# Product 5 of a convolution in two halves: 256-column units, then 512-column chunks of both sequences

## The chip, the cores and the metric

The kernel runs on one core of a Trainium2 chip. The metric is the device time in microseconds (us); lower is better. A core has a matrix engine (TensorE, PE in the profile; its weight loads are PEld), a vector engine (VectorE, DVE), an activation engine (ScalarE, ACT), a general engine (GpSimd, POOL) and a queue that issues most transfers (SyncE, SP). Matrix products are written to PSUM, which the kernel uses as 8 banks of 128 x 512 floats.

## The reference, cut to what matters

```python
x = x + attention(layernorm(x))          # x: 2 sequences x 1024 tokens x 1024
...
def attention(h):
    x = conv1d(h, conv_w, padding="SAME") + conv_b     # 3 taps, 1024 -> 768
    q, k, v = split(x, 3)
    # blocks of 128 tokens, 16 heads of 64, causal softmax, output projections
...
x = x + lora_linear(layernorm(x))        # 1024 -> 1024, 4 active experts
```

The change lies in the first third: the layer norm and the convolution with three taps over 1024 channels.

## The kernel before, in words

**The convolution as six products.** The tokens of each sequence are taken four at a time, and the convolution is computed from sums of shifted tokens times sums of taps, with six products per four tokens (numbered 0, 5, 1, 2, 3, 4 in the order they run) in place of twelve. Each product has 1024 input channels in 8 chunks of 128 (`NDC`), 768 output channels in 6 groups of 128 (`NCC`) and 256 columns for each of the two sequences (`J` = 256, `JN` = 512). A product therefore fills six PSUM banks, `pms[v, c]`, of 512 columns. For accuracy each operand is split into a rounded part and a remainder (`_hi` on ACT, `_lo` on DVE), and three matmuls stand for one: hi x hi, hi x lo, lo x hi (`three`).

**Two ways of multiplying.** Products 1 to 4 take a chunk of both sequences at once: 512 columns, 18 matmuls a chunk (`multiply`). Products 0 and 5 come first, while tokens are still being normalized and transposed, so they are cut into `units` (L464 on): one sequence, two chunks, 2 x 18 matmuls of 256 columns (`multiply_unit`). Units 0 to 7 are product 0, units 8 to 15 product 5. A unit's tokens are summed (`unit_sum`, DVE), rounded (`unit_hi`, ACT), and the remainder taken (`unit_lo`, DVE). Product 5 needs each chunk's weights for both sequences, so they stay in their buffers (a pool `t3` of 23) until the second sequence has passed.

**Tokens.** The input comes in 16 tiles of 128 tokens. Tiles 0 to 7 hold odd tokens (`xo`), tiles 8 to 15 even tokens (`xe`); 8 to 11 belong to the first sequence and 12 to 15 to the second. Each tile is normalized (statistics on DVE, scale on ACT) and transposed in two halves h = 0, 1 of 512 channels (chunks 0 to 3 and 4 to 7): a `turn(i, h)` is four PE transposes into a bank and one ACT copy (`transposed`, L399). The table `between` says after which half of which unit which turns come. Product 0 reads odd tokens only, product 5 even ones only, products 1 to 4 both.

**Products 1 to 4.** For products 1 and 2, and again for 3 and 4, DVE makes the sums of tokens of two chunks at a time, both sequences (`tokens_sum`, four instructions of 128 x 1024). Their `v_hi` and `v_lo` follow. The sums of taps are made by transfers that add to what is in place (`sum_g`, on POOL's queue) and by DVE (`combine`), then split by `u_hi` (ACT) and `u_lo` (DVE). A product's banks are emptied by ACT (`evacuate`) and stored (`spill`).

**The order.** Every step of the convolution is an `Op` with an engine, a planned time, a due time, a lead (how long ahead of its due time it may start) and the operations it waits for. `trace()` places them: over all engines it repeats the choice of the operation that can start earliest; on one engine, among those whose predecessors are placed, again the one that can start first, and of two equal ones the one due earlier. The instructions are then issued in the order of the planned starts, so on each engine this order is fixed; the chip runs it in order. An operation `tokens_sum` waits for `banks`, the list of all 32 copies of transposes. A second plan, after the convolution, orders attention and the second linear layer in the same way.

Of the kernel before, what the change touches and what calls it, by code (L numbers as in the profile page):

```python
# [10 lines left out]
F32 = mybir.dt.float32  # L11
# [5 lines left out]
ALU = mybir.AluOpType  # L17
# [22 lines left out]
def preln_block_kernel(  # L40
# [19 lines left out]
    nc = tc.nc  # L60
    N, L, D = x.shape
    C = conv_w.shape[2]
    NDC = D // P
    NCC = C // P
# [10 lines left out]
    J = L // 4  # L75
    JN = N * J
# [50 lines left out]
    def t4(name, shape, dt=FR):  # L127
        return t4p.tile([P, *shape], dt, tag="t4", name=name)
# [161 lines left out]
                t.append(sorted(places[k])[n - 1])  # L290
            return max(t, default=0.0)

    def trace():
        todo = {e: [o for o in plan if o.engine == e] for e in {o.engine: 0 for o in plan}}
        for ops in todo.values():
            ops.sort(key=lambda o: o.due)
        late = 0.0
        while any(todo.values()):
            best = None
            for e, ops in todo.items():  # L300
                held = None
                for o in ops:
                    t = o.earliest()
                    if t is None:
                        continue
                    t = max(free.get(e, 0.0), o.due - o.lead + late, t)
                    if o.port:
                        t = max(t, free.get("port", 0.0))
                    if held is None or t < held[0]:
                        held = (t, o)  # L310
                    if t <= free.get(e, 0.0):
                        break
                if held and (best is None or held[0] < best[0]):
                    best = held
            t, o = best
            o.start, o.end = t, t + o.takes
            free[o.engine] = o.end
            if o.port:
                free["port"] = o.end
            for k in o.need:  # L320
                places[k].remove(min(places[k]))
            for k in o.give:
                places[k].append(o.end + o.lag)
            todo[o.engine].remove(o)
            if o.engine == "PE":
                late = max(late, t - o.due)
        for o in sorted(plan, key=lambda o: o.start):
            o.f()
        plan.clear()
        return late  # L330
# [80 lines left out]
    raws, us, ukeep, vkeep, vts, pms = {}, {}, {}, {}, {}, {}  # L411
# [43 lines left out]
    def parts(dc, n):  # L455

        o, e = (
            t[:, dc, n, :] if isinstance(n, int) else t[:, dc].rearrange("p c n j -> p (c n) j")
            for t in (xo, home[0][0] if 0 in home else xo)
        )  # L460
        return (
            o[:, :, 0:J], e[:, :, 0:J], o[:, :, ds(J + 1, J)],
            e[:, :, ds(J + 1, J)], o[:, :, 1 : J + 1], e[:, :, 1 : J + 1],
        )  # L464


    units = [(v, n, dc) for v in (0, 5) for n in range(N) for dc in range(0, NDC, 2)]

    def unit_sum(q):

        v, n, dc = units[q]
        d = parts(ds(dc, 2), n)
        i = 0 if v == 0 else 1
        a = t2(f"va_{q}").rearrange("p (c j) -> p c j", c=2)
        nc.vector.scalar_tensor_tensor(a, d[i + 2], -5.0, d[i + 4], ALU.mult, ALU.add)
        nc.vector.scalar_tensor_tensor(a, d[i], 4.0, a, ALU.mult, ALU.add)
        vts[q] = a
# [6 lines left out]
    def unit_lo(q):  # L484
        a, vt = vts[q]
        nc.vector.tensor_tensor(vt[:, 1], a, vt[:, 0], ALU.subtract)
        vts[q] = [[vt[:, i, c, :] for i in range(2)] for c in range(2)]

    def tokens_sum(v, dc):


        d = parts(ds(dc, 2), None)
        a, b, kp = (t4(f"{n}_{v}_{dc}", (2 * N, J), F32) for n in ("va", "vb", "vkeep"))
        if v == 1:
            nc.vector.scalar_tensor_tensor(a, d[2], -4.0, d[4], ALU.mult, ALU.add)
            nc.vector.scalar_tensor_tensor(b, d[1], -4.0, d[3], ALU.mult, ALU.add)
            nc.vector.tensor_tensor(kp, a, b, ALU.subtract)
            nc.vector.tensor_tensor(a, a, b, ALU.add)
        else:
            nc.vector.tensor_tensor(a, d[4], d[2], ALU.subtract)  # L500
            nc.vector.tensor_tensor(b, d[3], d[1], ALU.subtract)
            nc.vector.scalar_tensor_tensor(kp, b, -2.0, a, ALU.mult, ALU.add)
            nc.vector.scalar_tensor_tensor(a, b, 2.0, a, ALU.mult, ALU.add)
        vkeep[v, dc], vkeep[v + 1, dc] = a, kp

    def v_hi(v, dc):
        hl = vts[v, dc] = [t4(f"v{i}_{v}_{dc}", (2 * N, J)) for i in range(2)]
# [26 lines left out]
    def mm(pm, v, dc, c, vt, first, last):  # L534
        three(pm, [u[:, ts(c, P)] for u in us[v, dc]], vt, first, last)

    def multiply_unit(q, i, c):
        v, n, dc = units[q]
        if (n, dc, i) == (0, 0, 0):
            pms[v, c] = bank(f"pm_{v}_{c}")  # L540
        mm(
            pms[v, c][:, ts(n, J)], v, dc + i, c, vts[q][i],
            dc + i == 0, dc + i == NDC - 1,
        )

    def multiply(v, dc, c):
        if dc == 0:
# [101 lines left out]
    HALF, TR = 2.15, 0.45  # L649
    DVE, ACT, PE, DMA = "DVE", "ACT", "PE", "DMA"  # L650
# [12 lines left out]
    at = [14.0]  # L663
    banks = []
    seen = {}
# [35 lines left out]
    for i in (6, 9):  # L701
# [9 lines left out]
    }  # L711

    idle = []
# [11 lines left out]
    last, ready = None, {}  # L725

    def evacuated(v, c, due):
        o = gone[v, c] = Op(ACT, 0.55 if v < 4 else 0.85, due, 3.0, [last], partial(evacuate, v, c))
        gone["m", v, c] = load(due, 3.0, spill, v, c, after=[o], takes=0.7)

    for q, (v, n, dc) in enumerate(units):
        base = 0 if v == 0 else 8
        took = [seen.get((base + 4 * n + i, dc // 4)) for i in range(4)]
        if None in took:
            for i in range(4):
                turn(base + 4 * n + i, dc // 4)
            took = [seen[base + 4 * n + i, dc // 4] for i in range(4)]
        due = at[0]
        if q == 0:

            Op(PE, 2.4, 16.9, 1.0, [seen["tr", 3, 0]], lambda: keep_busy(20))
        o = Op(DVE, 1.28, due - 5.5, 9.0, took, partial(unit_sum, q))
        o = Op(ACT, 0.55, due - 3.5, 9.0, [o], partial(unit_hi, q))
        side = Op(DVE, 0.64, due - 1.5, 9.0, [o], partial(unit_lo, q))
        for i in range(2):
            d = dc + i
            if n == 0:
                if v == 5:
                    gs[5, d] = load(at[0] - 12.0, 12.0, load_g, 5, d)
                ready[v, d] = weights_due(v, d, at[0], gs[v, d])  # L750
            for c in range(NCC):
                after = [last, side, ready[v, d]]
                if v == 5 and n == 0 and d == 0:
                    after.append(gone[0, max(0, c - 1)])
                last = Op(
                    PE, HALF / NCC, at[0], 6.0, after, partial(multiply_unit, q, i, c), lag=0.0
                )
                at[0] += HALF / NCC
            for j in between.get((q, i), []):
                turn(*j)  # L760
        if (n, dc) == (1, NDC - 2):
            for c in range(NCC):
                evacuated(v, c, at[0] + 0.1 * c)
    def begin_step(v, dc, due):
        if v in (1, 3):
            kept = Op(DVE, 4.7, due - 9.0, 22.0, banks, partial(tokens_sum, v, dc))
            gone["t", v, dc] = gone["t", v + 1, dc] = kept
        o = Op(ACT, 1.0, due - 5.0, 14.0, [gone["t", v, dc]], partial(v_hi, v, dc))
        return Op(DVE, 1.18, due - 3.0, 14.0, [o], partial(v_lo, v, dc))
# [31 lines left out]
    for v, dc in [(v, dc) for v in (1, 2, 3) for dc in range(0, NDC, 2)] + [(4, 0), (4, 2)]:  # L801
        if (v, dc) == (2, 0):

            for r in range(4):
                load(
                    at[0] + r, 3.0, nc.sync.dma_start, mask[r::4], causal[ts(r, P // 4)],
                    after=[last],
# [5 lines left out]
        for d in (dc, dc + 1):  # L813
            begin_chunk(v, d, at[0])
            for c in range(NCC):
                last = product(v, d, c, side)
# [14 lines left out]
    for c in range(NCC):  # L831
        got = load(
            at[0] - 4.0, 8.0, tokens_load, 0, c, t3, NV - 1,
            after=[gone["m", v, c] for v in (0, 5, 1, 2, 3)],
        )
        for d in range(NDC // 2, NDC):
            last = product(4, d, c, sides[d - d % 2])
        evacuated(4, c, at[0])
        o = Op(DVE, 2.7, at[0] + 1.0, 6.0, [got, gone[4, c]], partial(tokens_join, 0, c))
        o = Op(ACT, 0.6, at[0] + 4.0, 6.0, [o], partial(tokens_hi, 0, c))  # L840
# [3 lines left out]
    with tc.manual_schedule(  # L844
        engines={engines.DVE, engines.Activation, engines.PE, engines.SP, engines.Pool}
    ):
        nc.gpsimd.dma_start(bia, biases)
        Op(ACT, 0.2, 40.0, 3.0, [], lambda: nc.scalar.mul(bq8, bia[:, 0:NHP], SCALE))
        at[0] += trace()

    wqk, wvt, wot = par["wqk"], par["wv"], par["wo"]

# [576 lines left out]
    d = {}  # L1429
# [506 lines left out]
```

## Time and profile before

| | us |
|---|---|
| median of 3 runs | 752.37 (752.19 to 752.55) |
| the profiled execution | 752.35 |
| its span in the profile | 750.5 |
| first product to the end of product 4 (PE) | 18.78 to 230.03 |

| stretch, us | PE does |
|---|---|
| to 19 | transposes of tiles 0 to 3 and matmuls that only keep the engine busy |
| 19 to 61 | product 0, with transposes of tiles 4 to 11 |
| 61 to 99 | product 5, with transposes of tiles 12 to 15 |
| 99 to 230 | products 1, 2, 3, 4 |
| 230 to 750 | attention, output projection, the second layer norm and linear layer |

The span is what the profile records between the first and the last instruction; the rest of the time lies around it. A row of a timeline gives start, length (both us), engine, line, operation, the tile written and the tiles read, and in brackets how long the engine had been idle before it and what released it. Matmuls overlap, so their pace is read from the length of a run of them, not from the duration of one.

### The profile page before, as it was taken

The numbers are of one execution on the slowest core, as the hardware profiler recorded it, in microseconds if no ns is written. First come the engines' busy times: TensorE is split into PE (matmuls) and PEld (weight loads), VectorE is DVE, ScalarE is ACT, GpSimd is POOL, SyncE is SP. The second block draws the span as 40 slices with busy tenths as digits, with TensorE's granted clock in tenths as the row PEclk, the third lists the DMA queues.
The fourth block names the chain that finished last, engine by engine and source line by source line (L and its number), as shares of the span: only waits on it lengthen the run. The fifth ranks groups of instructions, "written<-read, shape, count | busy, mean of one in ns | idle before, by whom it ended". The sixth has DMA issues, their size and how long they took to land.

```text
span 750.5 us, 12939 instructions
## 1 busy us (share of the span) xinstructions
PE 741.9 (99%) x4746; PEld 633.9 (84%) x4746; DVE 596.3 (79%) x1051; ACT 421.3 (56%) x1044; POOL 187.4 (25%) x154
## 2 busy tenths in 40 slices
PE   8999999999999999999999999999999999999997
PEld 7999988888888888888888888888888888888886
DVE  6888899889767898898888888599667677577752
ACT  6888336464745998798898789863212212212120
POOL 3224321310000223132222312454142251331401
PEclk9999999999999999999999999999999999999999
DMA  9936994995753113363245344797655566565644
GB/s 342 379 104 206 248 267 107 292 287 124 249 167 127 44 50 103 132 220 103 99 153 206 131 151 138 266 386 317 227 211 225 215 238 235 209 225 217 227 174 168
DMA packets 65423, 149.46 MB, mean 199 GB/s; under 512 B 5918, under 2 KB 25006, under 8 KB 60240
## 3 DMA queue, kind: packets, MB, share of 16 engines
q1 hardware_dynamic: 61488, 138.51, 51.1%
q0 software_dynamic: 3728, 10.00, 7.4%
q8 instruction: 37, 0.61, 0.3%
q14 instruction: 26, 0.21, 0.1%
q10 hardware_dynamic: 144, 0.13, 0.1%
HBM read 114.01 MB, written 34.60 MB: 198 GB/s over the span
## 4 chain that ended last, share of the span: by engine, by line
PE 95%; DVE 2%; DMA 1%; ACT 1%; SPq 1%; issue 0%; DVEq 0%; ACTq 0%
PE pm L141 27%; PE pq L141 11%; PE py_c L1271 6%; PE pw L141 6%; PE py_a L1271 6%; PE pp L141 6%; PE py_e L1271 6%; PE pv L141 5%; PE po L978 4%; PE s L914 4%; PE pt L961 4%; PE py_b L1271 3%; PE pz L1288 2%; PE trx L1211 2%; PE tr L393 1%; DMA xt<-in_x 1%
## 5 line engine op out<-in xcount | busy, mean ns | idle before, releaser
L141 PE MATMUL pm<-v,u 128*128 128x256 f32 (+1 forms) x1152 | 203.1, 337 | 1.2 <-ACT v L481 0.6
L141 PEld LDWEIGHTS pm<-v,u 128*128 128x128 f32 x1152 | 177.8, 189 | 24.0 <-ACT v L481 0.9
L954 POOL TENSOR_TENSOR p<-p,rs 128x1024 f32<-128x1024 f32 x32 | 60.7, 1908 | 250.4 <-DVE rs L950 240.5
L943 ACT ACTIVATE p<-p,nmx 128x128 f32<-128x128 f32 x256 | 99.7, 398 | 4.3 <-DVE nmx L938 4.1
L141 PE MATMUL pq<-yt,wqk 128*128 128x512 f32 x384 | 94.6, 398 | 0.0
L141 PEld LDWEIGHTS pq<-yt,wqk 128*128 128x128 f32 x384 | 70.3, 188 | 16.8 <-issue 1.9
L1174 POOL TENSOR_TENSOR xr<-xr,projb 128x1024 f32<-128x1024 f32 x16 | 38.8, 2426 | 113.2 <-DMA xr<-in_x 104.7
L943 ACT ACTIVATION_READ_ACCUMULATOR p<-p,nmx 128x1 f32 x256 | 50.2, 196 | 0.0
L929 DVE TENSOR_TENSOR p<-s,mask 128x512 f32<-128x512 f32 x64 | 42.4, 685 | 9.7 <-PE s L914 9.5
L141 PE MATMUL pw<-oT,wot 128*128 128x512 f32 x192 | 47.9, 397 | 0.0
L141 PE MATMUL pv<-wvt,yt 128*128 128x512 f32 x192 | 47.1, 395 | 0.0
L141 PEld LDWEIGHTS pv<-wvt,yt 128*128 128x128 f32 x192 | 36.0, 188 | 8.8
L141 PEld LDWEIGHTS pw<-oT,wot 128*128 128x128 f32 x192 | 35.9, 188 | 8.7 <-DVE oT L999 0.2
L431 POOL DMA_DIRECT2D g<-in_conv_w x24 | 21.3, 938 | 69.9 <-ACT g L427 36.2
L453 DVE TENSOR_TENSOR u<-g,u 128x768 fp32r<-128x768 f32 x40 | 37.5, 953 | 1.5 <-ACT u L449 1.4
L969 DVE COPY pT<-pt 128x512 f32<-128x512 f32 x32 | 21.8, 688 | 20.8 <-PE pt L961 20.8
L938 DVE TENSOR_REDUCE nmx<-p 128x8 f32<-128x1024 f32 x32 | 37.7, 1196 | 0.1
L1233 ACT COPY s<-trx 128x512 f32<-128x512 f32 x8 | 4.7, 588 | 56.9 <-PE trx L1211 56.9
L449 ACT CAST u<-g 128x768 fp32r<-128x768 f32 x40 | 32.7, 838 | 5.2 <-PE pm L141 4.8
L914 PEld LDWEIGHTS s<-qk,qk 64*128 64x128 f32 x512 | 30.1, 187 | 5.1 <-issue 2.3
L914 PE MATMUL s<-qk,qk 64*128 64x128 f32 x512 | 34.0, 280 | 0.0
L1369 ACT COPY u<-py_a 128x512 f32<-128x512 f32 x8 | 4.7, 588 | 51.9 <-PE py_a L1271 51.9
(206 smaller groups left out, 1532.6 us busy)
## 6 DMA issues: line engine op xcount, KB each, us to landing
wb_B<-wsd_B SPq DMA_DIRECT2D x32, 1024.0 KB, 7.1
g<-in_conv_w SPq DMA_DIRECT2D x48, 384.0 KB, 8.3
mdr<-m SPq DMA_DIRECT2D x36, 256.0 KB, 3.0
g<-in_conv_w POOLq DMA_DIRECT2D x24, 384.0 KB, 7.3
xt<-in_x SPq DMA_DIRECT2D x16, 512.0 KB, 9.8
xr<-in_x SPq DMA_DIRECT2D x16, 512.0 KB, 5.6
out<-xr SPq DMA_DIRECT2D x14, 512.0 KB, 6.5
ml<-mdr SPq DMA_DIRECT2D x18, 384.0 KB, 4.0
```

Source lines behind the costliest of these rows:

```text
L141: nc.tensor.matmul(ps, l[a], r[b], start=first and i == 0, stop=last and i == 2)
L449: nc.scalar.copy(us[v, dc][0], raws[v, dc])
L453: nc.vector.tensor_tensor(lo, raws.pop((v, dc)), hi, ALU.subtract)
L914: nc.tensor.matmul(s[j][:, b, :], qh[ts(j, DH), ts(b, P)], kh[ts(j, DH), ts(b, P)], start=True, stop=True,)
L929: nc.vector.tensor_tensor(ps[i][0][:, ts(j, NB), :], ss[i][j], mask[:, None, :].to_broadcast([P, NB, P]), ALU.add,)
L938: nc.vector.tensor_reduce(nmx, p, AX.X, ALU.max, negate=True)
L943: nc.scalar.activation(p[:, k, :], p[:, k, :], AF.Exp, bias=nmx[:, k : k + 1], accum_out=sm[:, k : k + 1],)
L954: nc.gpsimd.tensor_tensor(p, p, rs[:, :, None].to_broadcast([P, 2 * NB, P]), ALU.mult)
L961: nc.tensor.transpose(pt[:, ts(b, P)], ps[i][0][:, j * NB + b, :], ident)
L978: nc.tensor.matmul(po[ts(j, DH), ts(b, P)], vh[:, b, ds((i % 4) * P + j * DH, DH)], pT[:, j, ts(b, P)], start=True, stop=True,)
L1174: nc.gpsimd.tensor_tensor(xrs[g], xrs[g], pwt["b"], ALU.add)
L1271: nc.tensor.matmul(pys[m, b], l[x], r[y], start=opens and c == 0 and i == 0, stop=c == NH - 1 and i == 2, skip_group_check=not opens,)
```

## The change

Product 5 now runs in two parts. Its chunks 0 to 3 stay in units of one sequence and two chunks (units 8 to 11). Its chunks 4 to 7 become four units of one chunk of both sequences, 18 matmuls of 512 columns each (units 12 to 15, sequence `None`). [...] The turns move: half 0 of tiles 12 to 15 comes at units 7 and 8, one at a time, and half 1 of all even tiles at units 9 and 10. A `tokens_sum` becomes two operations of two instructions each. And `trace` gets a patience: in the convolution an operation is only preferred to one that is due more than 2 us earlier if it can start over 1 us before it.

```diff
-    def trace():
+    def trace(wait=0.0):
...
-                    if held is None or t < held[0]:
-                        held = (t, o)
+                    if held is None or t < held[0] - (wait if o.due > due + 2.0 else 0.0):
+                        held, due = (t, o), o.due
                     if t <= free.get(e, 0.0):
                         break
...
-    units = [(v, n, dc) for v in (0, 5) for n in range(N) for dc in range(0, NDC, 2)]
+    units = [
+        *((0, n, dc) for n in range(N) for dc in range(0, NDC, 2)),
+        *((5, n, dc) for n in range(N) for dc in range(0, NDC // 2, 2)),
+        *((5, None, d) for d in range(NDC // 2, NDC)),
+    ]
...
-        d = parts(ds(dc, 2), n)
+        d = parts(ds(dc, 1 if n is None else 2), n)
...
-    def tokens_sum(v, dc):
+        if units[q][1] is None:
+            vts[q] = [[vt[:, i].rearrange("p c j -> p (c j)") for i in range(2)]]
+
+    def tokens_sum(v, dc, part):
...
+        if (v, part) == (1, 0):
+            stt(a, d[2], -4.0, d[4], ALU.mult, ALU.add)
+            stt(b, d[1], -4.0, d[3], ALU.mult, ALU.add)
+        elif v == 1:
+            tt(kp, a, b, ALU.subtract)
+            tt(a, a, b, ALU.add)
...
-        mm(
-            pms[v, c][:, ts(n, J)], v, dc + i, c, vts[q][i],
-            dc + i == 0, dc + i == NDC - 1,
-        )
+        cols = slice(0, JN) if n is None else ts(n, J)
+
+        opens = dc + i == 0 and (v == 0 or n == 0)
+        mm(pms[v, c][:, cols], v, dc + i, c, vts[q][i], opens, dc + i == NDC - 1)
...
-        (6, 1): [(8, 1), (9, 1)], (7, 0): [(10, 1), (11, 1)],
-        (9, 1): [(12, 0), (13, 0)], (10, 0): [(14, 0), (15, 0)],
-        (10, 1): [(12, 1), (13, 1)], (11, 0): [(14, 1), (15, 1)],
+        (7, 0): [(12, 0)], (7, 1): [(13, 0)], (8, 0): [(14, 0)], (8, 1): [(15, 0)],
+        (9, 0): [(8, 1), (9, 1)], (9, 1): [(10, 1), (11, 1)],
+        (10, 0): [(12, 1), (13, 1)], (10, 1): [(14, 1), (15, 1)],
...
+        which = range(base, base + 8) if n is None else range(base + 4 * n, base + 4 * n + 4)
+        took = [seen[i, dc // 4] for i in which]
...
-            kept = Op(DVE, 4.7, due - 9.0, 22.0, banks, partial(tokens_sum, v, dc))
+            kept = Op(DVE, 2.35, due - 9.0, 22.0, banks, partial(tokens_sum, v, dc, 0))
+            kept = Op(DVE, 2.35, due - 6.5, 22.0, [kept], partial(tokens_sum, v, dc, 1))
...
-        at[0] += trace()
+        at[0] += trace(1.0)
```

More of the change, by code (lines that the diff above doesn't have):

```diff
@@ L300, in trace @@
             for e, ops in todo.items():
-                held = None
+                held, due = None, 0.0
                 for o in ops:
@@ L487, in unit_lo @@
         vts[q] = [[vt[:, i, c, :] for i in range(2)] for c in range(2)]
-    def tokens_sum(v, dc):
+        if units[q][1] is None:
+            vts[q] = [[vt[:, i].rearrange("p c j -> p (c j)") for i in range(2)]]
+    def tokens_sum(v, dc, part):
         d = parts(ds(dc, 2), None)
[L493 to L498, printed above, removed]
-        else:
[L500 to L504, printed above, removed]
+        if part == 0:
+            vkeep[v, dc] = tuple(t4(f"{n}_{v}_{dc}", (2 * N, J), F32) for n in ("va", "vb", "vkeep"))
+        a, b, kp = vkeep[v, dc]
+        stt, tt = nc.vector.scalar_tensor_tensor, nc.vector.tensor_tensor
+        if (v, part) == (1, 0):
[4 more added lines that the diff above has]
+            tt(a, a, b, ALU.add)
+        elif part == 0:
+            tt(a, d[4], d[2], ALU.subtract)
+            tt(b, d[3], d[1], ALU.subtract)
+        else:
+            stt(kp, b, -2.0, a, ALU.mult, ALU.add)
+            stt(a, b, 2.0, a, ALU.mult, ALU.add)
+        if part == 1:
+            vkeep[v, dc], vkeep[v + 1, dc] = a, kp
     def v_hi(v, dc):
@@ L732, in preln_block_kernel @@
         base = 0 if v == 0 else 8
[L733 to L737, printed above, removed]
+        which = range(base, base + 8) if n is None else range(base + 4 * n, base + 4 * n + 4)
+        took = [seen[i, dc // 4] for i in which]
         due = at[0]
@@ L744, in preln_block_kernel @@
         side = Op(DVE, 0.64, due - 1.5, 9.0, [o], partial(unit_lo, q))
-        for i in range(2):
+        took = HALF / (3 if n is None else NCC)
+        for i in range(1 if n is None else 2):
             d = dc + i
-            if n == 0:
+            if n != 1:
                 if v == 5:
@@ L754, in preln_block_kernel @@
                     after.append(gone[0, max(0, c - 1)])
[L755 to L758, printed above, removed]
+                last = Op(PE, took, at[0], 6.0, after, partial(multiply_unit, q, i, c), lag=0.0)
+                at[0] += took
             for j in between.get((q, i), []):
                 turn(*j)
-        if (n, dc) == (1, NDC - 2):
+        if (n, dc) in ((1, NDC - 2), (None, NDC - 1)):
             for c in range(NCC):
```

## The prediction

> **What bounds the kernel now.** I read the busy shares first, then the groups of instructions, then the chain of waits, then the VectorE (DVE) and ScalarE (ACT) timelines around product 5, where the change lies.
>
> ```profile
> PE 741.9 (99%) x4746; PEld 633.9 (84%) x4746; DVE 596.3 (79%) x1051; ACT 421.3 (56%) x1044; POOL 187.4 (25%) x154
> ```
>
> TensorE (PE) is busy in 99% of the span. The view of who waited for whom lists only four PE waits in all: 2.9 us at the start, 0.6 and 0.5 us before the first product, 0.6 us at 260 us. So only fewer PE cycles can bring a gain, and a loss comes from any operand that is late. In the chain of waits (start us, length us, what) the stretch of the change reads:
>
> ```profile
> 59.15 10.79 PE pm L141 x90
> 69.94 0.87 PE tr L393 x8
> ...
> 79.12 0.87 PE tr L393 x8
> ...
> 79.99 150.04 PE pm L141 x738
> ```
>
> From 19.70 to 230.03 us the chain is nothing but PE: products, transposes, no gap. VectorE is what feeds it, by stretches of 30 us (us, PE, PEld, DVE, ACT, POOL, clock, DMA):
>
> ```profile
> 50.00:80.00 30.00, 30.00 (x257) 29.89 (x257) 23.92 (x41) 22.73 (x37) 10.92 (x14) 1.00 0.77 218
> 80.00:110.00 30.00, 30.00 (x210) 28.11 (x210) 28.96 (x30) 11.68 (x18) 7.04 (x8) 1.00 1.03 261
> 110.00:140.00 30.00, 30.00 (x134) 24.86 (x133) 29.19 (x40) 18.55 (x24) 7.28 (x8) 1.00 0.63 170
> ```
>
> DVE is 80% busy up to 80 us and 97% from 80 to 140 us. There it is nearly a second bound, so the question is when it may begin the work of product 1. These rows of the two timelines show that:
>
> ```profile
> 79.59 1.08 ACT L399 COPY xe<-tr 128x512 f32<-128x512 f32 x2 [1.43 <-PE tr L393]
> ```
>
> ```profile
> 80.70 0.69 DVE L475 SCALAR_TENSOR_TENSOR va<-xe 128x512 f32<-128x512 f32 x1 [1.81 <-ACT xe L399]
> 83.96 1.22 DVE L495 SCALAR_TENSOR_TENSOR va<-xo 128x1024 f32<-128x1024 f32 x1
> ...
> 111.10 1.22 DVE L495 SCALAR_TENSOR_TENSOR va<-xo 128x1024 f32<-128x1024 f32 x1
> 117.17 1.23 DVE L512 TENSOR_TENSOR v<-va,v 128x1024 fp32r<-128x1024 f32 x1 [0.26 <-ACT v L508]
> 118.32 0.95 DVE L453 TENSOR_TENSOR u<-g,u 128x768 fp32r<-128x768 f32 x1
> ```
>
> The last copy of a transpose ends at 79.59 + 1.08 = 80.67. Only then can the last units be summed, and the plan lets no `tokens_sum` start before all copies are done. From 83.96 to 123 us DVE is idle for 0.26 us in all.
>
> **Fewer matmuls.** Product 5 had 8 units of 36 matmuls of 256 columns. The second half of its chunks, 144 matmuls, becomes 72 of 512. The 256-column pace is 10.79 us / 90 = 119.9 ns. The last piece of the chain holds 9 x 18 = 162 of these, 19.42 us, and 576 of 512 columns, so those take (150.04 - 19.42)/576 = 226.8 ns. Two small ones cost 239.8 ns, one large one 226.8 ns: 72 x 13.0 ns = **0.93 us saved**, all on the path. [...]
>
> The second edit of the multiplication, no opening flag for the second sequence of product 5, costs nothing: the same matmul with another flag.
>
> **Transposes moved.** Product 1 of the old run starts at 79.99 + 19.42 = 99.41, the new one at 98.48. All 16 groups of the even tokens stay (8 transposes take 0.87). But the last group now stands before unit 11 and the four wide units, 4.32 + 16.33 = 20.65 us before product 1, so it ends at 77.83 and its copies 0.68 later, at 78.51 (before 80.67). Tiles 12 to 15 are needed at 57 to 65 us rather than 70 to 73. Their statistics run at 58.6 to 66.6 now and would have to move into 46 to 54. Beside them stand the splits of product 5's weights (four between 47.6 and 57.4), which are not read before 61 to 68 and can give way, and DVE idles 2.7 us there: nothing on the path. Price if that fails: one chain from statistics to scaled tile, some 4 us (1.65 for the statistics, 0.9 + 0.4 on POOL, 1.25 for the scale).
>
> **The switch from product 0 to 5.** Now tile 13 is transposed exactly there, and its copy stands in ACT's queue behind the first evacuation. The six evacuations ran from 59.72 at 0.51 us each with no stranger among them. With one 0.53 us copy in front of the other five, which waits for a transpose that ends near 60.4, evacuations two to five end at 61.5 to 63.0. PE wants its banks from 61.2 to 62.3 (0.36 us apart); two spare banks help, one of which the transpose holds. Between 0 and 0.85 us of stall; I take **0.4**.
>
> **The first wide unit.** Its sum can start at 78.51; the chain sum 1.33, the next sum 1.33 in front of its split, split 0.69, and 0.1 for signals gives 81.96, and PE comes at 77.83 + 4.32 = 82.15. It just fits: 0, at most 0.3.
>
> **VectorE in product 1.** Four units now need the last transposes where two did before. Start-to-start in DVE's timeline: a unit's sum 1.33, its split 0.61, a whole `tokens_sum` 4.83 (4.79 to 4.87), split of v 1.13, a combination of weights 0.87, split of u 0.87. From 78.51 to the point where chunk 6 of product 1 is ready: 4 x (1.33 + 0.61) + one late split of product 5's weights 0.87 + 4 x 4.83 + 4 x 1.13 + 8 x 0.87 + 7 x 0.87 = 45.5 us, thus 124.0. PE reaches chunk 6 (six chunks of 18 x 226.8 ns = 4.08 us) at 98.48 + 24.49 and reads the split in its second matmul, at 123.2. **Late by 0.8 us.** The old run by the same sum has 40.8 us from 80.67, 121.4 against 124.1: 2.7 us of room. That room is spent by two more units (3.9), a weight split (0.9) and the faster PE (0.9), less the 2.2 us by which the copies end earlier. DVE will be idle before 78 instead, about 10 us, since nothing else may start there.
>
> The two pieces help in order, not in amount. In the old run the sum at 111.10 (4.87 us) stood in front of the split at 118.32, used near 120.3. Divided, the second piece is due 0.1 us after that split, so the split moves ahead; chunk 5 is then ready at 118.7 against 119.3. Bounds of the product 1 stall: 0, if the last combination of weights goes behind and ACT is quick, to 2.1, if weight combinations hold the queue as well; I take **0.6**.
>
> **The plan's patience of 1 us.** It acts on the whole convolution. At the start it changes little: the operation worth waiting for is mostly not placed yet when DVE chooses, so the waits of 0.6 and 0.5 us stay (bounds: 0.3 gained, 0.3 lost). In product 3 the split at 176.05 is read near 177.4, with a `tokens_sum` at 171.26 in front; patience and pieces should bring it forward, which covers the 0.9 us by which PE comes earlier. Behind 230.03 nothing is edited; the plan there is made anew from the same relative times: 0, with ±0.5 for another order.
>
> **Sum**, against the profiled execution, 752.35 (span 750.5 and 1.85 around it): -0.93 + 0.4 + 0.6 = +0.07, hence **752.4 us**; the median of the runs shown, 752.37, is the same within 0.02.
>
> **Rivals.**
> *Clean gain.* No stall at the switch or in product 1: 752.35 - 0.93 = 751.4. For it: PE never waited between 20 and 230 us, ACT idles a lot, weights for product 1 can be loaded earlier since product 5 frees them earlier. Against it: the DVE sum.
> *Slower: the patience idles VectorE in product 1.* From 84 to 123 us DVE has no time to give. If the plan holds it for each of the four splits of v that wait for ACT (1.06 us for the cast plus signals, less one short operation that fits), 0.7 us each, all 2.8 us go to PE: 752.4 + 2.8 = 755.2. For it: the rule is blind to how loaded an engine is. Against: mostly a short operation with a near due time is ready, and the rule lets that go first. It decides from 1.4 us of such idling on (then the time is above 753.9).
> *The change doesn't do what it says.* If the wide units ran at twice the small pace, nothing is saved and the stalls stay: 753.3. Products 1 to 4 already run at the wide pace, so this is small.
>
> **Chances.** Forecast (0.4 to 1.8 us given back, 751.6 to 753.4) 0.42; clean gain 0.23; slower 0.30; no saving 0.05. The range 751.2 to 755.4 takes in the clean gain and the slower case's value. Faster by over 0.2% would need 1.5 us where 0.93 is to be had: 0.04. Within: 0.62. Slower: 0.34, the slower case and the upper end of the forecast.
>
> **What would show it.** Right: 72 fewer matmuls, product 5 shorter by 0.9; the last copy of the even tokens near 78.5; DVE idle between 54 and 78 and full after it; PE waits at L141 on DVE v or u between 115 and 125 us, and on ACT m near 61. Wrong: no PE wait at all there (751.4), or DVE idle between 84 and 123 with PE waits of over 2 us.

## The result, and the profile after

The changed kernel takes **757.28 us** (median of 5 runs, 755.91 to 757.6) where the kernel before takes 752.37. The ratio is 1.0054, with a 95% interval of 1.0043 to 1.0066: slower by 4.9 us, outside the range that was predicted (751.2 to 755.4). The profiled execution took 757.6 us, with a span of 755.8.

The busy shares of the page after the change:

```profile
PE 742.6 (98%) x4674; PEld 630.1 (83%) x4674; DVE 591.3 (78%) x1051; ACT 421.3 (56%) x1044; POOL 186.7 (25%) x154
```

The 72 matmuls are gone (4746 to 4674), so the change does what it says. The view by stretches (us, PE, PEld, DVE, ACT, POOL, clock, DMA share, GB/s) shows where PE lost time:

```profile
50.00:80.00 30.00, 29.87 (x250) 29.31 (x249) 19.82 (x34) 23.02 (x37) 7.55 (x12) 1.00 0.59 186
80.00:110.00 30.00, 27.77 (x132) 22.79 (x131) 26.13 (x30) 11.54 (x17) 8.96 (x11) 1.00 1.07 279
110.00:140.00 30.00, 27.68 (x119) 22.37 (x120) 28.21 (x39) 16.94 (x22) 5.13 (x6) 1.00 0.58 151
```

PE is idle for 2.2 and 2.3 us in the two later stretches, where it was never idle before. DVE does *less* between 80 and 110 us than it did (26.13, before 28.96), although the prediction had it as the full engine there. So something starved DVE. PE's own timeline names the operands that it waited for, in brackets ahead of which it was idle:

```profile
97.20 12.53 PE L141 MATMUL pm<-v,u 128*128 128x512 f32 x54 [1.96 <-DVE v L492]
110.75 0.50 PE L141 MATMUL pm<-v,u 128*128 128x512 f32 x1 [1.02 <-DVE v L526]
111.62 12.55 PE L141 MATMUL pm<-v,u 128*128 128x512 f32 x54 [0.37 <-DVE u L454]
125.37 4.83 PE L141 MATMUL pm<-v,u 128*128 128x512 f32 x20 [1.20 <-DVE u L454]
```

That is 4.55 us in four waits. The first is for the remainder of the last wide unit. The chain of waits (start, length, what) leads from it back to a transfer, where the old chain had only PE:

```profile
72.40 2.06 PE pm L141 x18
74.46 13.53 DMA g<-in_conv_w
...
88.81 0.62 ACT v L487
```

A load of weights (g) that PE's freeing of a buffer released at 74.46 us took 13.5 us. Three timelines tell why it came so late and whom it held. First SP, the queue that issues loads and stores:

```profile
44.69 0.33 SPq L421 DMA_DIRECT2D g<-in_conv_w  x1
60.68 4.59 SPq L544 DMA_DIRECT2D mdr<-m  x6
65.36 0.41 SPq L424 DMA_DIRECT2D g<-in_conv_w  x1
...
67.51 0.85 SPq L421 DMA_DIRECT2D g<-in_conv_w  x2
...
74.46 0.33 SPq L421 DMA_DIRECT2D g<-in_conv_w  x1
```

L421 loads weights for products 0 and 5, L424 and L425 for product 1, and L544 is the spill of a finished product. After 44.69 SP stands in front of product 0's spills and waits for their evacuation until 60.68. Everything behind them waits too: 10 loads are then issued within 5.2 us, and the last of product 5's, `g(5,7)`, stands behind eight of product 1's and waits for a buffer besides. In the kernel before, all eight loads of product 5 were issued by 51 us, ahead of the spills, as its row shows; here only five were.

```profile
24.62 26.39 SPq L420 DMA_DIRECT2D g<-in_conv_w  x8
```

Then ACT, which rounds the weights (L450) and the units (L487), and DVE:

```profile
78.04 1.07 ACT L400 COPY xe<-tr 128x512 f32<-128x512 f32 x2 [1.22 <-PE tr L394]
...
88.07 0.83 ACT L450 CAST u<-g 128x768 fp32r<-128x768 f32 x1 [5.51 <-DMA g<-in_conv_w]
88.81 1.14 ACT L487 CAST v<-va 128x512 fp32r<-128x512 f32 x2
```

```profile
85.07 0.69 DVE L482 SCALAR_TENSOR_TENSOR va<-xe,va 128x512 f32<-128x512 f32 x1
89.45 0.69 DVE L492 TENSOR_TENSOR v<-va,v 128x512 fp32r<-128x512 f32 x1 [3.70 <-ACT v L487]
...
96.46 0.68 DVE L492 TENSOR_TENSOR v<-va,v 128x512 fp32r<-128x512 f32 x1
```

The rounding of `g(5,7)` holds ACT for 5.51 us. The roundings of the last two wide units, whose sums were ready at 85.8, stand behind it; DVE stands idle for 3.70 us for want of them, and everything that DVE has to do for product 1 begins that much later. The remainder that PE waits for is made at 96.46, behind a sum for product 1.

A count by pace agrees. Unit 11 starts at 78.44 (counted as the prediction counted, from the end of the transposes ahead of it), 0.61 later than predicted. From there 36 matmuls of 119.9 ns and 648 of 226.8 ns would end at 229.72, but the convolution ends at 235.37: 5.65 us of stalls. Together with the 0.61 and less the 0.93 saved, that is the 5.3 us by which it ends later than before (230.03). The waits listed are 4.55 of it. The rest fits the last matmul ahead of each wait: on record it lasts 0.50 us (the row at 110.75), 0.27 more than the pace, and four times that is 1.1.

### The profile page after: what moved, and what is told of

The parts are those of the page before. It is cut to its first block, busy times and chain, and to the rows that moved or that the text cites. A ratio compares the mean times of both kernels' runs of the same rounds, so it can differ in the third digit from the quotient of the medians.

```text
span 755.8 us, 12795 instructions
## 1 busy us (share of the span) xinstructions
PE 742.6 (98%) x4674; PEld 630.1 (83%) x4674; DVE 591.3 (78%) x1051; ACT 421.3 (56%) x1044; POOL 186.7 (25%) x154
## 4 chain that ended last, share of the span: by engine, by line
PE 88%; DVE 6%; DMA 2%; ACT 1%; issue 1%; POOL 0%; DVEq 0%; ACTq 0%
PE pm L141 21%; PE pq L141 11%; PE py_c L1283 6%; PE pw L141 6%; PE py_a L1283 6%; PE pp L141 6%; PE py_e L1283 6%; PE pv L141 5%; PE po L990 4%; PE s L926 4%; PE pt L973 4%; PE py_b L1283 3%; PE pz L1300 2%; PE trx L1223 2%; DMA g<-in_conv_w 2%
## 5 line engine op out<-in xcount | busy, mean ns | idle before, releaser
L141 PE MATMUL pm<-v,u 128*128 128x512 f32 (+1 forms) x1080 | 204.4, 349 | 5.6 <-DVE v L492 2.9
L141 PEld LDWEIGHTS pm<-v,u 128*128 128x128 f32 x1080 | 174.2, 189 | 33.0 <-DVE v L492 3.5
L450 ACT CAST u<-g 128x768 fp32r<-128x768 f32 x40 | 32.6, 835 | 15.4 <-PE pm L141 7.8
```

Of the source, the lines that this page charges most:

```text
L141: nc.tensor.matmul(ps, l[a], r[b], start=first and i == 0, stop=last and i == 2)
L450: nc.scalar.copy(us[v, dc][0], raws[v, dc])
```

## The experiments

Ratios are to the kernel before, measured on the same chip beside each group of runs, with their 95% intervals. The kernel before had medians of 752.48 (x runs), 752.83 (y runs) and 753.27 (z runs), so times of different groups are compared by their ratios. The fastest executions of the kernel before agree in all three groups (751.75, 751.86 and 751.85); what moves its median is their scatter, up to 756.8. The ratios contain that scatter, so where they and the medians of the runs disagree, both are given.

### The loads of product 5's weights

**x1**: the changed kernel, with the loads of the four wide chunks due 22 us earlier, ahead of the spills.

```diff
-gs[5, d] = load(at[0] - 12.0, 12.0, load_g, 5, d)
+gs[5, d] = load(at[0] - (34.0 if n is None else 12.0), 12.0, load_g, 5, d)
```

> The changed kernel, but the four weight loads of product 5's chunks 4 to 7 are due 34 us before their chunk instead of 12, so that SP issues them ahead of product 0's six spills, as the kernel before did. Theory A (blocked queue: the load of chunk 7's weights comes late, its rounding on ACT stands in front of two roundings of token sums, and VectorE idles 3.7 us behind it): VectorE's idle of 3.7 us near 86 to 89 us is gone and about 3.7 us come back, 753.6 +- 0.8. Theory B (patience of 1 us orders product 1 badly): no more than 1 us comes back, 756.3 to 757.3. Theory C (the prediction's: too much VectorE work after the last transposes): the idle may go, and what is left over the kernel before is PE waits in product 1 of 0.8 to 2 us; 752.2 to 754.

Measured: 754.34 us, ratio 1.0026 [1.0017, 1.0034]. 2.9 of the 4.9 us are back by the medians; by the ratios, whose excess falls from 0.54% to 0.26%, about half of the loss. This lies in theory A's range. SP's timeline of this run has all eight loads of product 5 ahead of the spills:

```profile
24.91 18.16 SPq L421 DMA_DIRECT2D g<-in_conv_w  x8
60.92 4.29 SPq L544 DMA_DIRECT2D mdr<-m  x6
```

DVE is then full from 79.40 to past 126 us but for 0.39 and 0.25 us, and the wait of 1.96 is gone. PE's timeline has two left in product 1, 1.66 us in all, within the 0.8 to 2 of theory C:

```profile
108.58 12.53 PE L141 MATMUL pm<-v,u 128*128 128x512 f32 x54 [0.37 <-DVE u L454]
122.41 7.77 PE L141 MATMUL pm<-v,u 128*128 128x512 f32 x33 [1.29 <-DVE u L454]
```

**x2**: the loads as in the changed kernel; only the rounding of `g(5,7)` may no longer be placed early, so that the units' roundings go first.

```diff
-o = Op(ACT, 0.76, due - 5.0, 12.0, [after], partial(u_hi, v, d))
+o = Op(ACT, 0.76, due - 5.0, 3.0 if (v, d) == (5, 7) else 12.0, [after], partial(u_hi, v, d))
```

> The changed kernel with one number changed: the rounding of chunk 7's weights in product 5 may start at most 3 us ahead of its due time instead of 12, so ACT's queue has it behind the roundings of units 14 and 15. The load itself stays late (lands near 88 us). Theory A: the late load then hurts nobody, the same 3.7 us come back as in the run with early loads, 753.6 +- 0.8. If it is instead the saturated transfers (late weights of product 1) that hurt: no gain, 757.

Measured: 756.2, ratio 1.0045 [1.0032, 1.0058]. Theory A fails here: the idle of 3.70 is gone, and yet only 1.1 us came back by the medians, and the interval overlaps that of the changed kernel. The loads of product 1 that stand in the same burst now hold DVE (2.05 us at 106.52), and PE waits for it:

```profile
110.94 0.50 PE L141 MATMUL pm<-v,u 128*128 128x512 f32 x1 [1.63 <-DVE v L526]
```

So the blocked queue on ACT is one of two ways in which the late loads act. x1 takes away the first and most of the second (DVE stands 0.39 us there). How much of the lateness of `g(5,7)` is the blocked SP, the wait for a buffer or the slow landing was not tested separately.

### The patience

**x3**: the changed kernel without patience.

```diff
-at[0] += trace(1.0)
+at[0] += trace()
```

> The changed kernel with the patience of trace() set back to 0. Theory B: most of the 4.9 us come back, 752.4 to 753.5. Theory A: ACT's queue still has chunk 7's rounding in front of roundings of token sums, and the load is as late: 756 to 758.5, and the PE waits in product 1 stay.

Measured: 755.69, ratio 1.0043 [1.003, 1.0056], 1.6 us back by the medians, between the two theories and with an interval that overlaps that of the changed kernel. Besides, this run can't be read for patience alone: the plan also orders the loads otherwise, `g(5,7)` lands at 82.7 in place of 88.0, and DVE idles only 1.77 us for it. Therefore **z1**: x1 without patience, with the loads early in both.

> x1_loads_before_spills with the plan's patience taken out: the weight loads of the wide chunks stand ahead of the spills in both, so the load order that blurred x3_no_patience should differ less. Theory (patience is harmless or helps a little): 754.3, within 0.5 of x1 (754.34). Rival (patience idles VectorE or ACT for the sake of later operations): 1 us or more back, 753.3 or less.

Measured: 753.96, ratio 1.0008 [0.9999, 1.0017], against x1's 1.0026. The profiled executions differ by 0.9 (753.74 and 754.65), the ratios by 1.3 us, the medians of the two groups by 0.4. By the medians this is the theory, by the ratios the rival. Where it comes from is to be seen in the order on DVE. With patience (x1), ahead of the split that PE waits for at 122.41:

```profile
118.15 1.22 DVE L509 TENSOR_TENSOR vkeep<-va,vb 128x1024 f32<-128x1024 f32 x1
119.39 1.23 DVE L510 TENSOR_TENSOR va<-va,vb 128x1024 f32<-128x1024 f32 x1
120.54 0.95 DVE L440 SCALAR_TENSOR_TENSOR g<-g,g 128x768 f32<-128x768 f32 x1
121.41 0.95 DVE L454 TENSOR_TENSOR u<-g,u 128x768 fp32r<-128x768 f32 x1
```

and without it (z1):

```profile
118.05 1.23 DVE L510 TENSOR_TENSOR va<-va,vb 128x1024 f32<-128x1024 f32 x1
119.20 0.95 DVE L454 TENSOR_TENSOR u<-g,u 128x768 fp32r<-128x768 f32 x1
120.06 0.95 DVE L440 SCALAR_TENSOR_TENSOR g<-g,g 128x768 f32<-128x768 f32 x1
```

The split comes 2.2 us earlier. Most of it is accounted for: 0.87 since a combination of weights no longer stands in front of it, 0.64 since DVE no longer idles 0.39 and 0.25, 0.44 since the whole stretch began earlier. PE then waits 0.36 us in product 1. So patience does cost, between 0.4 and 1.3 us, and by the order of the operations more than by an idle engine. z1 has a wait of 0.69 us at 231.18 in return, for an evacuation behind product 4.

### The pieces

**x4**: the kernel before, with the sums in two pieces and with patience, but with small units throughout.

> The kernel before with the tokens' sums in two pieces and the patience of 1 us, but with product 5 in its old units and the transposes in their old places. Theory A and C: the loss belongs to the wide units, so this one is at 752.4 +- 0.7. Theory B: slower by 2 us or more.

Measured: 753.31, ratio 1.0015 [1.0, 1.0029]. Its trace has no wait in product 1. Most of the 4.9 us therefore needs the wide units or the turns that moved with them, which this run leaves out together.

**z2**: x1 with the sums whole again.

```diff
-kept = Op(DVE, 2.35, due - 9.0, 22.0, banks, partial(tokens_sum, v, dc, 0))
-kept = Op(DVE, 2.35, due - 6.5, 22.0, [kept], partial(tokens_sum, v, dc, 1))
+kept = Op(DVE, 4.7, due - 9.0, 22.0, banks, lambda: [tokens_sum(v, dc, k) for k in range(2)])
```

> x1_loads_before_spills with the sums of the tokens' side planned as one operation again. Theory (the pieces do not bring the split of chunk 5 of product 1 ahead, since its combination of weights is planned late): same time as x1, 754.3 within 0.5, and the PE wait on DVE u near 122 us stays near 1.3 us. Rival (the prediction's: the pieces hold the wait down): that wait grows by 1 us or more and the time goes to 755.3 or above.

Measured: 757.1, ratio 1.0047 [1.0032, 1.0062]. The theory falls: the pieces help, by 1.6 us by the ratios and 2.8 by the medians, part of which is a lower clock after the wait (0.57 from 112 to 116 us in the profiled execution; last section). The place is another one, as PE's timeline shows:

```profile
110.67 0.50 PE L141 MATMUL pm<-v,u 128*128 128x512 f32 x1 [3.26 <-DVE v L526]
```

The whole sum at 104.61 stands in front of the split of v of chunks 2 and 3 (109.40), and PE waits 3.26 us for that. In x1 that split goes between the two pieces of this sum (106.45) and costs PE nothing there.

### The width alone

**z3**: x1 with only chunks 6 and 7 wide, and the turns of the even tokens behind units 6 to 10, none at the switch between products.

```diff
-*((5, n, dc) for n in range(N) for dc in range(0, NDC // 2, 2)),
-*((5, None, d) for d in range(NDC // 2, NDC)),
+*((5, n, dc) for n in range(N) for dc in range(0, NDC - 2, 2)),
+*((5, None, d) for d in range(NDC - 2, NDC)),
...
-(7, 0): [(12, 0)], (7, 1): [(13, 0)], (8, 0): [(14, 0)], (8, 1): [(15, 0)],
-(9, 0): [(8, 1), (9, 1)], (9, 1): [(10, 1), (11, 1)],
-(10, 0): [(12, 1), (13, 1)], (10, 1): [(14, 1), (15, 1)],
+(6, 1): [(8, 1), (9, 1)], (7, 0): [(10, 1), (11, 1)],
+(8, 1): [(12, 0), (13, 0)], (9, 0): [(14, 0), (15, 0)],
+(9, 1): [(12, 1), (13, 1)], (10, 0): [(14, 1), (15, 1)],
```

> x1_loads_before_spills with only chunks 6 and 7 of product 5 multiplied wide, the even tokens' turns back behind units 6 to 10 (none at the switch from product 0 to 5, as in the kernel before). Expected saving of PE time half of 0.93 us, 0.46. Theory (the loss of x1 is the switch, about 0.9, plus VectorE's lateness in product 1): the switch costs nothing again and two more units, not four, need the last transposes, whose copies end about as early: 752.0 to 752.8, same as before. Rival (the pieces and the patience cost by themselves, as x4_before_pieces_patience's 0.8 hints): 753 to 754.

Measured: 752.34 us (751.9 to 752.74, 11 runs), ratio 0.9984 [0.9975, 0.9993], as its theory said. This is the fastest version of the study: about 5 us below the changed kernel, and 0.16% below the kernel before, which had 753.27 beside it. The interval leaves out 1, but the margin is smaller than the 0.2% from which the prediction counts a kernel as faster, and the profiled execution (752.5) is no faster than that of the kernel before (752.35). Nor is its fastest one (751.9, against 751.85); what is smaller is the scatter. z3 changes the number of wide chunks and the turns together, so it doesn't tell which of the two made x1's loss go. From 50 to 140 us PE has no wait:

```profile
80.00:110.00 30.00, 30.00 (x179) 26.82 (x178) 29.73 (x31) 11.51 (x16) 8.56 (x10) 1.00 1.07 271
110.00:140.00 30.00, 30.00 (x134) 24.82 (x133) 26.70 (x37) 18.29 (x24) 5.20 (x6) 1.00 0.57 155
```

**z4**: z3 with whole sums and no patience.

> z3_two_wide_chunks with whole sums and no patience: the kernel before with two wide chunks, earlier turns and early loads only. If the wide chunks as such are harmless: 751.9 (752.4 less 0.46), at most the same as before. If turns or loads collide anyway: 753 or more, with PE waits on ACT m or DVE u to show where.

Measured: 756.91, ratio 1.0039 [1.0026, 1.0051]. The first alternative misses by 5 us, and the second holds. With two wide chunks, pieces and patience *together* are worth 4.6 us by the medians, a lower clock among it (the profiled execution has two spells, with 0.50 and 0.64 in the stretches of 2 us from 20 to 24 us and 0.84, 0.50 and 0.81 in those from 104 to 110). PE waits 1.95 us at 104.56 for an evacuation of product 5. The evacuations (103.92 on) stand on ACT behind a rounding at 102.24 that waited 7.92 us for a whole sum on DVE. In z3 the plan puts the evacuations (96.41) ahead of that rounding (100.30).

### The switch from product 0 to product 5

**y1** and **y4** are x1 with the turns at the switch elsewhere.

```diff
-(7, 0): [(12, 0)], (7, 1): [(13, 0)], (8, 0): [(14, 0)], (8, 1): [(15, 0)],
+(7, 0): [(12, 0), (13, 0)], (8, 1): [(14, 0), (15, 0)],
```

> The run with early loads (754.34), and no transposes at the switch from product 0 to product 5: tile 13 is turned together with tile 12 in unit 7, tiles 14 and 15 together after unit 8; the last transposes stay where they are. If the copy among the evacuations costs what the trace shows there (about 0.9 us between 60 and 66 us), 0.9 us come back: 753.4, and PE starts unit 11 about 0.9 us earlier. If that delay only lets VectorE catch up (it works off the same amount before product 1 whatever PE does), the waits in product 1 grow by the same 0.9 us and the time stays at 754.3.

```diff
-(7, 0): [(12, 0)], (7, 1): [(13, 0)], (8, 0): [(14, 0)], (8, 1): [(15, 0)],
-(9, 0): [(8, 1), (9, 1)], (9, 1): [(10, 1), (11, 1)],
-(10, 0): [(12, 1), (13, 1)], (10, 1): [(14, 1), (15, 1)],
+(7, 0): [(12, 0), (13, 0)], (8, 0): [(14, 0), (15, 0)],
+(8, 1): [(8, 1), (9, 1)], (9, 0): [(10, 1), (11, 1)],
+(9, 1): [(12, 1), (13, 1)], (10, 0): [(14, 1), (15, 1)],
```

> The run with early loads, all turns of the even tiles earlier: tiles 12 and 13 in unit 7, 14 and 15 after the first half of unit 8, and the last transposes after the first half of unit 10 instead of its second half, with none at the switch. The last copies end about 2.2 us earlier, 77 instead of 79.4. Theory C with the switch: 0.9 us at the switch and the 1.7 us of waits in product 1 go, 751.4 to 752.2, at or below the kernel before. If VectorE's start does not decide: 753.4.

Measured: 755.64, ratio 1.0034 [1.002, 1.0048], and 755.74, ratio 1.0033 [1.0019, 1.0048]. Both are misses, 1.3 and 1.4 us worse than x1 by the medians (0.6 and 0.5 by the ratios). In y1 the scale of tile 15 (59.85) now stands in front of the evacuations on ACT, the sixth evacuation waits 2.40 us for the landing of a spill, and the last copy ends later, not earlier (80.73, against 79.37 in x1). In y4 the scales again stand there (57.50 and 59.59, the evacuations from 61.46), and PE waits 0.56 and 0.85 us for evacuations. Moving two turns moves their statistics and scales as well, to where ACT is busy with the evacuations (61.00 to 63.52 in y1, 61.46 to 64.01 in y4, for the first five). The cost of the switch itself was therefore not isolated; the pace count gives about 0.9 us for it in the changed kernel.

### DVE's room in product 1

**y2**: x1 with one subtraction less in each of the four sums of product 1. The kernel leaves out the difference that product 2 needs and multiplies `b` in its place, so it serves for its time alone.

```diff
-tt(kp, a, b, ALU.subtract)
...
-vkeep[v, dc], vkeep[v + 1, dc] = a, kp
+vkeep[v, dc], vkeep[v + 1, dc] = a, b if v == 1 else kp
```

> The run with early loads, and VectorE spared four instructions of 1.25 us in product 1: the difference that product 2 uses is left out (product 2 multiplies one of the two sums instead). Theory C (VectorE has too much work after the last transposes): three of them stand before the split that PE waits for at 122.4, so that PE wait of 1.3 us and the one of 0.4 us vanish, 752.6 +- 0.4. If the waits come from weights that land late, not from VectorE's load: no gain, 754.3.

Measured: 753.07, ratio 0.9992 [0.9978, 1.0005]. With 5 us less for DVE to do, 1.3 us come back by the medians (2.6 us by the ratios), and the wait of 1.29 at 122 us is gone. Waits of 0.44 and 0.36 us near 108 stay, for a split of v and one of u on DVE; why these come late with less for DVE to do is not shown.

**y3**: the kernel *before*, with that subtraction issued twice in three of the sums, 3.7 us more for DVE.

```diff
-nc.vector.tensor_tensor(kp, a, b, ALU.subtract)
+for _ in range(2 if dc < 6 else 1):
+    nc.vector.tensor_tensor(kp, a, b, ALU.subtract)
```

> The kernel before, with one instruction of each of the first three sums of product 1's tokens issued twice (3 x 1.25 = 3.7 us more for VectorE between 84 and 107 us, the same order of all instructions). The prediction's sum gives the kernel before 2.7 us of room at chunk 6, its trace about 1.0 us at the split for chunk 5. So theory C: PE waits 1.0 to 2.7 us in product 1, 753.4 to 755.1. If VectorE's load in product 1 does not matter: 752.4.

Measured: 756.45, ratio 1.0043 [1.0026, 1.006]. The kernel before has almost no room: two of the three extra subtractions (2.5 us) are done by 103 us, and PE waits 2.17 us there, for an evacuation that stands on ACT behind a rounding that waits for DVE. In the kernel before, ACT had the same order, without a wait of PE:

```profile
98.13 1.06 ACT L508 CAST v<-va 128x1024 fp32r<-128x1024 f32 x1 [6.61 <-DVE va L498]
99.83 3.03 ACT L524 ACTIVATE m<-pm 128x512 f32<-128x512 f32 x6
```

In y3 the chain of waits has the rounding at 100.93 and the evacuation that PE waited for from 102.71. PE's timeline of y3, and the stretches around it:

```profile
103.26 5.07 PE L141 MATMUL pm<-v,u 128*128 128x512 f32 x14 [2.17 <-ACT m L525]
```

```profile
102.00:104.00 2.00, 0.74 (x3) 0.66 (x4) 2.00 (x3) 2.00 (x4) 0.87 (x1) 1.00 1.06 263
104.00:106.00 2.00, 2.00 (x7) 1.52 (x7) 2.00 (x3) 2.00 (x5) 0.88 (x1) 0.59 1.04 332
106.00:108.00 2.00, 2.00 (x7) 1.57 (x6) 1.97 (x3) 0.36 (x1) 0.00 (x0) 0.56 1.08 297
108.00:110.00 2.00, 2.00 (x10) 1.62 (x9) 1.97 (x2) 0.00 (x0) 0.87 (x1) 1.00 1.08 294
```

The wait isn't all: after it PE runs 7 matmuls in 2 us in place of 10, at a granted clock of 0.59 and 0.56. That is another (0.41 + 0.44) x 2 = 1.7 us, so the 4.2 us by which this execution (756.57) is longer than that of the kernel before are 2.17 of wait, 1.7 of clock and 0.3 of the rest, which fits the 0.27 of a last matmul ahead of a wait.

## Why the prediction was wrong, by its own steps

The step that failed is the one on VectorE in product 1: it summed DVE's work and took for granted that DVE is fed. In the measured run DVE stood idle for 3.70 us instead, behind a load of product 5's weights that came late, and PE's four waits were 4.55 us where 0.6 was taken. The prediction's own sign of being wrong, DVE idle between 84 and 123 us with PE waits of over 2 us, came true.

- **Fewer matmuls**, 0.93 saved: right. 72 are gone, and at the wide pace the rest of the convolution would have ended at 229.72.
- **Transposes moved**: nearly right. The last copy ends at 78.04 + 1.07 = 79.11 (predicted 78.51), and DVE idles before it as predicted (4.10, 2.50 and 1.23 us are its longest idles between 62 and 77).
- **The switch**: 0.4 was taken, with 0.85 as the upper bound; about 0.9 was paid, by the count of pace from 60.22 to 78.44. The mechanism was right, the size was at its end: one copy at 61.03 stood between the second and third evacuation.
- **The first wide unit**, 0: it had no listed wait; its sum and PE both came some 0.6 us later than predicted.
- **VectorE in product 1**, 0.6: what failed is its list of what DVE needs. "One late split of product 5's weights 0.87" was priced as DVE time alone; the load and the rounding ahead of that split were not followed. The change makes the weights of four chunks needed later, those of chunk 7 by half a unit and three wide chunks, 2.2 + 12.2 = 14.4 us; since a load is planned 12 us ahead of its use, this puts the later of their loads behind the six blocked spills on SP, into a burst with product 1's loads. Advancing those loads gives 2.9 us back by the medians (x1); without it, even a freed ACT gives only 1.1 (x2).
- The same step's **room** of 2.7 us in the old run was too large: a sum over DVE's work up to chunk 6 missed that product 5's evacuations wait on ACT for DVE at 103 us, where the room was at most about 2.5 - 2.17 = 0.3 us (y3). With the loads early, DVE's lateness shows as waits of 0.37 and 1.29 us, not 0.6.
- **The two pieces** were said to bring the split of chunk 5 ahead. They don't: in the changed kernel both pieces (from 117.96 and from 121.10) and a combination (123.50) still stand in front of it (124.36). They help elsewhere, at the split of v (z2).
- **The plan's patience**, 0, and its rival of 755.2: 0.4 to 1.3 us in product 1 (z1 against x1). The rival had the right place, at least twice the price, and not the main mechanism: order more than idling (idles of 0.64 us in all, and not all of them the patience's). It does not explain the 757.3, which x1 brings to 754.3 with the patience in place.
- **Clean gain** argued that weights for product 1 could be loaded earlier, as product 5 frees buffers earlier. The reverse held: product 5's loads came later and took their places in the queue among product 1's.

The sum of what was shown, by the medians of the runs: of 4.9 us, 2.9 goes with the late loads (x1), 0.4 with patience (z1 against x1), and 1.6 is left for the switch and DVE's lateness less the 0.93 us saved. By the excess of the ratios the same parts are 2.1, 1.3 and 0.6 us, the last with an interval that holds 0. So the late loads are the largest part by either measure; the sizes of the other two are not settled. The parts also depend on each other: whole sums cost 1.6 to 2.8 us with patience (z2), and whole sums without patience 4.6 (z4). Not settled are the cost of the switch by itself, width against moved turns, and why the plan with two wide chunks is better with both pieces and patience than with neither, beyond the order on ACT that z4 shows.

## What to carry to other kernels

When a step is moved, follow each of its operands back to the instruction that issues the load, and ask what stands in front of that instruction in its queue: here a store that waited for a result held every load behind it on SP for some 16 us, whatever their due times. A sum over a busy engine says how late it is if it is fed; it says nothing of when it is fed, and one order of its queue can have far less room than the sum has (here at most about 0.3 us by y3, against 2.7). And compare what a change saves with what it moves: 0.93 us of matmuls did not pay for the new places of turns and loads, and the version with two wide chunks and no turn at the switch lost nothing, but gained nothing measurable either.

## What the hardware showed that was not expected

**A wait of 2 us can cost nearly twice its length.** In y3, a wait of 2.17 us was followed by 3.4 us at a granted clock of 0.5 (by half microseconds, from about 104.4 to 107.8), 1.7 us more. The same is seen after the 3.26 us in z2 (0.57 from 112 to 116 us), the 1.95 us in z4 (0.84, 0.50 and 0.81 in the stretches of 2 us from 104 to 110) and the 1.63 us in x2 (0.72, 0.50 and 0.93 in those from 112 to 118; there with 0.37 more half a microsecond later), but in the profiled execution of the changed kernel the 1.96 us at 97.20 left the clock at 1.00. The executions of z2 and z4 divide accordingly: the four with a mean granted clock of 0.999 or above took 754.87 to 755.44 us, the fourteen below it 756.53 to 758.01. So of the 757 us of these two kernels some 2 us go with this clock. Why a wait of 1.63 us had the effect in x2 and one of 1.96 us in the changed kernel had not, no run here shows.

**A load that takes 8 us can take 13.** The profile's page has a median of 9.6 us from issue to landing for these loads (8.3 before); the one issued at 74.46, within a stretch in which the DMA engines were busy throughout (share 1.01 to 1.09 from 74 to 90 us, by stretches of 2 us), took 13.5.

**ACT's queue held what was ready, as SP's did.** ACT had two roundings whose inputs were ready by 85.8 us and stood until 88.07 at one whose input was not. In the same way evacuations stood behind a rounding that waited for DVE in y3 (100.93, the evacuation that PE waited for from 102.71) and in z4 (102.24, the evacuations from 103.92).
